# Gated cross-attention and a quantized feed-forward layer on one core: order of the value matrices, form of the last softmax, place of the row statistics and size of the last norms

## The chip, the core and the metric

The kernel runs on one core of a Trainium2 chip. The metric is the device time of one execution in microseconds (us), as the median of several runs of the same program. A profile is one execution of its own, recorded by the hardware profiler. The engines are named as in the profile: PE is TensorE (matrix multiplications and transposes), DVE is VectorE, ACT is ScalarE, POOL is GpSimd, and SP is SyncE, which issues most of the transfers.

## What is computed

The input `x` has 4 batches of 1024 tokens of 512 features. The context has 64 rows of 512 features for each batch. All data are float32.

```python
def _layernorm(x, axis=-1, eps=1e-05):
    m = jnp.mean(x, axis=axis, keepdims=True)
    v = jnp.var(x, axis=axis, keepdims=True)
    return (x - m) / jnp.sqrt(v + eps)

# cross-attention: 16 heads of 64; scores * 64**-0.5, -10000 where key > query
weights = jax.nn.softmax(scores, axis=-1)
out = jnp.einsum('bhqk,bhkd->bhqd', weights, v)
return out.transpose(0, 2, 1, 3).reshape(bsz, q_len, HEADS * HEAD_DIM) @ w_o

# feed-forward: every act_qdq takes one largest value over the whole tensor
x = act_qdq(x)
up = act_qdq(x @ lpbq_dequant(w_up).T)
gate = act_qdq(x @ lpbq_dequant(w_gate).T)
sig = fixed_qdq_u16(jax.nn.sigmoid(gate))
gate = act_qdq(gate * sig)
o = act_qdq(gate * up)
return o @ lpbq_dequant(w_down).T

x = x + jnp.tanh(g_xattn[0]) * _L0_xattn_ref(_layernorm(x, axis=-1), ctx_1024, ctx_1024, ...)
x = x + jnp.tanh(g_ffn[0]) * _L0_ffn_ref(_layernorm(x, axis=-1), ...)
```

## The kernel before

The 4096 tokens are 32 tiles of 128 rows. Two tiles make a pair `q` (16 pairs, 4 for each batch) and four tiles make a group `g` (8 groups). The keys are folded into the query weights (`m_all`, one matrix for each batch) and the output weights into the values (`vwo`, one for each batch), so that attention for a pair is two products of 512 by 1024 and 1024 by 512. Each product is done by a seven-product scheme of the Strassen kind. The sums that it needs are made on DVE: `batch_sums` for the side of a batch (L398 to L403, four steps over 128x1024 elements), `score_left` for the tokens (L373 to L376) and `weights_turned` for the softmax weights (L665 to L668).

**Set-up (to about 75 us).** The weights are loaded and multiplied, and `m_all` is made for all batches. `value_matrix` (L608) makes a 128x512 piece of `vwo` from two matmuls. Each multiplies 64 rows of context into 64 output rows, and so fills one quarter of the array. For even batches the two lie on the quarters of one diagonal, for odd batches on those of the other. Batches 2 and 3 are made in one loop, a piece of one beside a piece of the other, and stored to DRAM for later. A piece goes from PSUM to SBUF on ACT (L614) or DVE (L616).

**Attention (to about 560 us).** The loop over `q` overlaps pairs. `scores(q + 1)` runs the seven products of the next pair on PE in the order 1, 6, 2, 5, 7, 3, 4. Each result leaves PSUM by an ACT copy (L426) or a DVE addition (L428). After chosen products PE does other work: the transposes of the softmax weights of pair `q` (`turn`, L659, copied by ACT at L661) and the transposes of the centred tokens of pair `q + 2` (`next_left`, L369). Those tokens were centred by ACT (L356) with the mean and deviation of the first norm. For batches 0 and 1 the pieces of `vwo` are made behind products of the first two score blocks: eight pieces of batch 0 during `scores(0)`, eight of batch 1 during `scores(1)`, each time two pieces of the same batch together.

`softmax(q + 1, ...)` follows. For each tile DVE takes the largest score of each head (L444). For the first pair the rest is done in large steps: subtraction (L448), one exponential over 128x1024 (L451), sums (L452). For all others ACT does 16 exponentials, one for each head, with the bias and sum in the instruction (L456). A reciprocal (L461) and a product (L462) end both forms.

`attend(q, ...)` runs seven products for the output in the order 1, 6, 2, 7, 5, 4, 3. They share three PSUM regions, so a product must wait until the result before it in its region was added to `xg` on DVE (L701). Products 6, 7 and 4 follow one another in the region `oq`. At its end the statistics of the two finished tiles are taken (`stats`, L321 and L324).

**Norms.** `norm_of` turns variances into reciprocal deviations. It adds epsilon on DVE (L173), takes a square root on ACT (L176, for which ACT loads another function table), and does six small steps on DVE (L178 to L186). One call can serve a finished group (second norm) and a coming group (first norm) together. For groups 1 to 4 the statistics of the first norm are taken early in set-up; for groups 5, 6 and 7 `group_stats` takes them in the loop at `q` = 7, 9 and 11, and the `norm_of` at the end of that pass uses them.

**After the last pair** the last two tiles are normalized by one `norm_of`, scaled on DVE (L726), their largest value taken (L729) and transposed (L734). The largest value over all tokens (L195 on DVE, L197 across partitions on POOL) gives `inv_x`. Gate and up products (24 units of seven products each), quantization with their own global maxima, and the down projection (from about 1210 us) follow. `token_side` rounds the tokens (L926 and L927 on DVE, L932 and L933 on ACT) and makes the sums of the gate stage (L956 to L965). `weight_sums` (L303 to L306) makes those of the weights: four of six during the last attention, the other two at the call of the first `token_side`.

The order on PE in the loop is the program's. On the other engines a scheduler orders the instructions when the program is built, by its own estimate of times. `tc.high_priority(SOON)` moves an instruction ahead in that order, `tc.issue_after(added)` forbids the instructions in it to stand before the instruction `added`, which is the last addition of `attend`. Each engine then works through its list strictly in order.

## Time and profile before

| quantity | value |
|---|---|
| median of three runs | 1469.01 us (1468.62 to 1470.72) |
| profiled execution | 1470.09 us, of which 1468.3 us are the span of the instructions |
| PE busy | 1423.3 us, 97% of the span |
| DVE busy | 1131.6 us, 77% |
| ACT busy | 688.0 us, 47% |
| mean granted clock of PE | 0.99 |

The span is counted from the first to the last instruction. An entry of a timeline gives its start, its length, engine, line, operation, what it writes and reads, and in brackets how long its engine sat idle before it and what ended that. A matmul in float32 shows as two or more records; the distance from one start to the next tells what it costs. The granted clock is the share of full speed at which PE was allowed to run.

### The profile page before, as it was taken

Reading aid. Unit: us, or ns where it says so; the run is one execution under the profiler, and the core shown is the slowest. Engines: PE = TensorE matmul, PEld = TensorE weight load, DVE = VectorE, ACT = ScalarE, POOL = GpSimd, SP = SyncE. Lnnn points to the kernel's source line nnn. Section 1 sums busy time; section 2 is a strip of 40 time slices with the busy share of each in tenths; the row PEclk is TensorE's granted clock in tenths of the full one; section 3 lists DMA queues with packets and bytes.
Section 4 is the critical chain, followed back from the end, with each engine's and each line's share of the span. In section 5 each row is a group of like instructions: output and inputs, shape, how many; then the busy total and the mean of one; then the engine's idle time right before and its main releaser. Section 6 shows DMA issues by size and latency. Waiting matters only on the chain. (4 is left out here: it accounts for less than half of the span.)

```text
span 1468.3 us, 15353 instructions
## 1 busy us (share of the span) xinstructions
PE 1423.3 (97%) x4944; PEld 863.1 (59%) x4944; DVE 1131.6 (77%) x2071; ACT 688.0 (47%) x1734; POOL 97.5 (7%) x191
## 2 busy tenths in 40 slices
PE   8999999999999988999999999999999899999999
PEld 6636776666676674444444444444444448888887
DVE  2855888988988888799975569888888897666632
ACT  2645777777677562010000049977776532222200
POOL 0000000000000002000000000000000101111110
PEclk9999999999999999999999999999999999999999
DMA  9541232432322235862322439958557474554421
GB/s 329 208 139 41 72 96 91 155 122 69 129 60 85 96 67 212 266 263 86 129 86 108 150 133 343 368 216 314 215 215 258 172 271 173 187 187 173 141 73 44
DMA packets 121402, 240.14 MB, mean 164 GB/s; under 512 B 57700, under 2 KB 57956, under 8 KB 115300
## 3 DMA queue, kind: packets, MB, share of 16 engines
q1 hardware_dynamic: 95844, 137.39, 28.1%
q0 software_dynamic: 18560, 76.56, 13.4%
q10 hardware_dynamic: 6912, 25.17, 4.2%
q8 instruction: 39, 0.64, 0.2%
q14 instruction: 47, 0.39, 0.1%
HBM read 130.03 MB, written 109.05 MB: 163 GB/s over the span
## 5 line engine op out<-in xcount | busy, mean ns | idle before, releaser
L456 ACT ACTIVATE e<-e,mx 128x64 f32<-128x64 f32 x480 | 159.5, 336 | 3.4 <-DVE mx L454 3.3
L863 PE MATMUL pqup<-t,wuT 128*128 128x512 f32 x192 | 92.5, 604 | 5.6 <-DVE raw_up L884 2.7
L428 DVE TENSOR_TENSOR e<-s,e 128x512 f32<-128x512 f32 x80 | 54.8, 685 | 55.2 <-PE s L420 54.9
L420 PE MATMUL s<-t,xs 128*128 128x512 f32 x192 | 91.9, 602 | 2.2 <-DVE xs L374 2.2
L456 ACT ACTIVATION_READ_ACCUMULATOR e<-e,mx 128x1 f32 x480 | 90.9, 189 | 0.0
L879 ACT COPY raw_gate<-ppgate 128x512 f32<-128x512 f32 x24 | 14.0, 585 | 144.7 <-PE ppgate L863 144.7
L1388 PE MATMUL ep<-wdT,upe 128*128 128x256 f32 x336 | 77.1, 379 | 0.0
L1314 ACT ACTIVATE uie<-upe,inv_up 128x1024 int16<-128x1024 f32 x48 | 53.7, 1145 | 48.7 <-DVE upe L1318 28.7
L1388 PE MATMUL eq<-tw,upe 128*128 128x256 f32 x312 | 72.4, 379 | 0.0
L1388 PEld LDWEIGHTS ep<-wdT,upe 128*128 128x128 f32 x336 | 63.8, 190 | 9.1 <-issue 0.5
L1087 ACT ACTIVATE gi<-gt,inv_gate 128x1024 int16<-128x1024 f32 x48 | 54.9, 1143 | 30.0 <-DVE q L1097 29.7
L863 PEld LDWEIGHTS pqup<-t,wuT 128*128 128x128 f32 x192 | 34.5, 189 | 57.8 <-issue 29.7
L863 PE MATMUL ppup<-xu,wuT 128*128 128x512 f32 x144 | 67.7, 592 | 0.0
L693 PE MATMUL oq<-t,eT 128*128 128x256 f32 x256 | 62.3, 387 | 5.2 <-DVE xg L701 5.2
L871 ACT COPY raw_gate<-ppgate 128x512 f32<-128x512 f32 x24 | 14.0, 585 | 108.4 <-PE ppgate L863 77.9
L1388 PEld LDWEIGHTS eq<-tw,upe 128*128 128x128 f32 x312 | 59.3, 190 | 8.1
L1318 DVE SCALAR_TENSOR_TENSOR upe<-uie,inv_o,gse 128x1024 f32<-128x1024 int16 (+1 forms) x50 | 60.5, 1233 | 3.0 <-ACT uie L1314 2.7
L420 PE MATMUL s<-m_all,xs 128*128 128x512 f32 x128 | 59.7, 598 | 1.2 <-DVE vwo L616 0.9
L863 PE MATMUL pqgate<-t,wgTb 128*128 128x512 f32 x128 | 60.4, 594 | 0.0
L420 PEld LDWEIGHTS s<-t,xs 128*128 128x128 f32 x192 | 35.4, 192 | 42.3 <-issue 39.3
L420 PE MATMUL s<-mb,xs 128*128 128x512 f32 x128 | 58.9, 592 | 0.0
L989 DVE TENSOR_REDUCE am_gate<-raw_gate 128x1 f32<-128x1024 f32 x48 | 58.2, 1212 | 0.8
(339 smaller groups left out, 3151.3 us busy)
## 6 DMA issues: line engine op xcount, KB each, us to landing
gate_d<-raw_gate ACTq DMA_DIRECT2D x48, 512.0 KB, 2.6
gt<-gate_d SPq DMA_DIRECT2D x48, 512.0 KB, 4.9
upe<-up_d SPq DMA_DIRECT2D x24, 1024.0 KB, 6.3
up_d<-raw_up POOLq DMA_DIRECT2D x46, 512.0 KB, 3.6
gse<-gsi_d SPq DMA_DIRECT2D x24, 512.0 KB, 4.4
gsi_d<-q SPq DMA_DIRECT2D x44, 256.0 KB, 4.0
xg<-in_x_dram SPq DMA_DIRECT2D x8, 1024.0 KB, 6.5
x_d<-xg POOLq DMA_DIRECT2D x32, 256.0 KB, 2.3
```

What stands on the lines that cost most here:

```text
L420: nc.tensor.matmul(bank[at], a[k][:, h, :], b[k][:, h, :], start=start and h == 0, stop=h == HC // 2 - 1, skip_group_check=True,)
L428: nc.vector.tensor_tensor(dst, bank[at], other, add)
L456: nc.scalar.activation(ei[:, h, :], ei[:, h, :], AF.Exp, bias=mx[:, h : h + 1], accum_out=sm[:, h : h + 1],)
L693: nc.tensor.matmul(bank[at], a[k][:, h, :], b[k][:, h, :], start=start and h == 0, stop=h == HP // 2 - 1, skip_group_check=True,)
L863: nc.tensor.matmul(bank[at], a[k][:, h, :], b[k][:, h, :], start=start and h == 0, stop=h == HC // 2 - 1, skip_group_check=True,)
L871: nc.scalar.copy(r0[:, 1, :], bank["pp"])
L879: nc.scalar.copy(r0[:, 0, :], bank["pp"])
L989: nc.vector.tensor_reduce(am_gate[:, u : u + 1], rf, AX.X, ALU.max, apply_absolute_value=True)
L1087: nc.scalar.activation(gi, g, AF.Copy, scale=inv_g)
L1314: nc.scalar.activation(ui, up[:, i, :], AF.Copy, scale=inv_u)
L1318: ins = nc.vector.scalar_tensor_tensor(o[:, i, w], ui[:, w], c_o, gs[:, i, w], ALU.mult, ALU.mult)
L1388: nc.tensor.matmul(bank[at], a[u // 2][k][:, u % 2, q % 2, :], w_of[u // 2][k][:, u % 2, :], start=start and u == 0, stop=u == UPB - 1, sk ...
```

## The change

Five places are edited. The matrices of batches 0 and 1 are made together, one piece of each at a time, behind five products of `scores(0)` and three of `scores(1)`; the two halves of `batch_sums(0, 1)` and the transposes of pair 1 move accordingly. The softmax of the last tile takes the large steps of the first pair. `group_stats` for groups 5 to 7 comes after the last addition of `attend`. The last two tiles get a `norm_of` each. The last two `weight_sums` for the gate come after the sums of `token_side`.

```diff
@@ softmax
-            if q == 0:
+            if q == 0 or t == NT - 1:
@@ values of batches 0 and 1
-        values_done = [0, 0]
-        def values_of(b, n):
-            def some():
-                for _ in range(n):
-                    hp = values_done[b]
-                    values_done[b] += 1
-                    value_matrix(
-                        b, hp, ps_o.tile([P, H], F32, name=f"ps_vo{b}_{hp}", tag=("opn", "oq")[hp % 2])
-                    )
-            return some
+        values_done = iter(range(HP))
+        def values(then=lambda: None):
+            hp = next(values_done)
+            for b, at in ((0, "opn"), (1, "oq")):
+                value_matrix(b, hp, ps_o.tile([P, H], F32, name=f"ps_vo{b}_{hp}", tag=at))
+            then()
@@ ahead of the loop
-        ahead = scores(0, dict.fromkeys((6, 2, 5, 7), values_of(0, 2)), score_banks(0))
+        ahead = scores(
+            0, {6: values, 2: values, 5: lambda: values(lambda: next_left(1)), 7: values, 3: values},
+            score_banks(0),
+        )
+        softmax(0, ahead)
         firsts = batch_sums(0, 1)
-        next(firsts)
-        softmax(0, ahead)
-        next_left(1)
@@ in the loop, scores of the next pair
-                    behind = {**dict.fromkeys((1, 6, 2, 5), values_of(1, 2)), 3: turn, 4: behind[3]}
+                    behind = {**dict.fromkeys((1, 6, 2), values), 3: turn, 4: behind[3]}
                 ahead = scores(q + 1, behind, score_banks(q + 1))
+                if q == 0:
+                    next(firsts)
                 softmax(q + 1, ahead)
@@ in the loop, around attend
                 load_group(q // 2 + 2)
-                if q // 2 + 2 > 4:
-                    group_stats(pa, q // 2 + 2, xg[q // 2 + 2])
...
             added = attend(q, a[0])
             with tc.issue_after(added):
+                if q % 2 == 1 and 4 < q // 2 + 2 < NG:
+                    group_stats(pa, q // 2 + 2, xg[q // 2 + 2])
                 if b + 1 < B and k in (1, QPB - 1):
                     for _ in batch_sums(b + 1, k // 2):
                         pass
@@ after the loop
-        norm_of(pa, [second_norm(slice(last + 2, NT))], "c2")
+        for t in (NT - 1, NT - 2):
+            norm_of(pa, [second_norm(slice(t, t + 1))], f"c{t}")
+        renormed(NT - 1)
         renormed(NT - 2)
-        renormed(NT - 1)
@@ gate stage
-                nc.vector.tensor_tensor(t[3], x0[:, HI, :], t[1], sub)
+                summed.append(nc.vector.tensor_tensor(t[3], x0[:, HI, :], t[1], sub))
...
-                    for p in range(len(ag), UPB):
-                        ag.append(weight_sums(wgT, sg_t, p, "g"))
+                    with tc.issue_after(summed[-1].ins):
+                        for p in range(len(ag), UPB):
+                            ag.append(weight_sums(wgT, sg_t, p, "g"))
```

More of the change, by code (lines that the diff above doesn't have):

```diff
@@ L923 @@
         with tc.tile_pool(name="pb", bufs=2) as pb:
+            summed = []
             def on_dve(tb, h):
```

## The prediction

> **What bounds the kernel now.** I read the busy times first, then what PE waited for, then the timelines around those waits.

> ```profile
> PE 1423.3 (97%) x4944; PEld 863.1 (59%) x4944; DVE 1131.6 (77%) x2071; ACT 688.0 (47%) x1734; POOL 97.5 (7%) x191
> ```

> PE is the bound, and 45 us of the 1468.3 us span are idle on it. An edit can shorten PE's own work, or remove a wait of PE. The waits of PE from 75 to 600 us (total us, how often, longest) are what the edits aim at:

> ```profile
> PE oq L693 <- DVE xg L701: 5.2, 3, 2.0
> PE ps_xm L734 <- DVE xm L726: 4.1, 1, 4.1
> PE ps_e L659 <- DVE e L462: 3.9, 1, 3.9
> PE ppgate L863 <- ACT xi L932: 2.8, 1, 2.8
> PE s L420 <- DVE xs L374: 2.2, 1, 2.2
> ```

> A wait costs more than its length if the clock drops behind it. Three stretches show when (length, PE busy, granted clock):

> ```profile
> 325.15:328.56 3.41, 1.85 (x9) 1.00 0.60 94
> 441.20:444.60 3.40, 1.41 (x7) 1.00 0.95 133
> 444.60:448.00 3.40, 3.40 (x10) 0.51 0.87 354
> ```

> All times below are on the clock of the profiled execution (span 1468.3 us, 1470.09 us in all, 1.1 us above the median of 1469.01 us). Differences are applied to the median.

> **Values side by side: gain.** The first pair of lines is four pieces, two of batch 2 and two of batch 3. The second is two pieces of one batch.

> ```profile
> 64.28 1.95 PE L608 MATMUL ps_vo<-wo_sb,vT 64*64 64x512 f32 x16
> 66.16 1.09 PE L369 MATMUL ps_xn<-ident,xn 128*128 128x128 f32 x8
> ...
> 78.81 1.93 PE L608 MATMUL ps_vo<-wo_sb,vT 64*64 64x512 f32 x8
> 80.68 1.98 PE L420 MATMUL s<-m_all,xs 128*128 128x512 f32 x4
> ```

> Start to start, four pieces take 1.88 us beside one another and two pieces 1.87 us. Two pieces of different batches thus cost 0.94 us; eight groups save 8 x 0.93 = 7.5 us. The wait on L374 (2.2 us), a short one of 0.2 us and the slow stretch at 103.3 (1.7 us) go too, since the token sums now stand ahead of the softmax on DVE: 11.6 us.

> Two new waits take from this. First, ACT's new order puts the exponential of tile 1 between the two evictions of the sixth group. `scores(1)` would start at 93.9. DVE gets product 3 at 91.2 and does two additions (0.6 us start to start), mask, two maxima and two subtractions (1.15 to 1.2 us): 98.3. The exponential ends at 99.9 and the second eviction (0.65) at 100.6. PE is ready for group seven at 98.5; its halves run at 99.0 and 100.65 and not together, which costs 2.2 us. Second, `batch_sums(0, 1)` now stands on DVE behind L665. From the arrival of the softmax weights (124.29 before) the list is L665, L398, L666, L667, L668, L373, L399: four at 0.60, 1.14, 0.34 and 1.22 us end at 129.4. Product 6 of `attend(0)` needs L399 and is due at 126.05: 3.4 us of wait. Over all phases that loses 0 to 3.4 us of clock, mean 1.9. Part: 11.6 - 2.2 - 3.4 - 1.9 = **4.1 us gained** (2.5 to 6).

> [...]

> **Last softmax in large steps: gain.** PE waits 3.94 us and then runs at half speed:

> ```profile
> 537.85 1.94 PE L659 MATMUL ps_e<-ident,e 128*128 128x128 f32 x8 [3.94 <-DVE e L462]
> ```

> 16 exponentials with their reads (0.33 us start to start, 5.3 us) become one of about 1.0 us, and DVE gets L448 and L452 (1.2 us each). In the new order, exponentials of tile 30 end at 529.9, tile 31's at 530.9. DVE does L462 of tile 30 (to 531.5), L452, an addition, L461, L321, an addition, and L462 (1.22): 535.2. PE waits 1.6 us, which does not drop the clock. Transposes (two times 0.87) and product 1 (1.73) follow, and product 6 of the last `attend` starts at 538.9, not 544.18: **5.3 us gained** (3.5 if the wait passes 2 us).

> **Last norm by tiles, late weight sums: gain.** The added second norm is seven small steps at 0.2 us or less and one square root of 0.2 us. Without four L303 to L306 pairs, and with tile 31's chain begun before the last addition, my walk has the last L729 end at 560.0, not 561.3. The rest of the chain to `inv_x` is unchanged. PE stays idle enough to start the gate slow as now: **1.3 us gained** (0 to 2.5). The moved sums fit before L884, and units 4 and 5 need them 48 us later: nothing. The tokens' L926 and L927 of the next pair also move back and are needed 70 us later: nothing.

> **Statistics behind the additions: loss.** The three waits on L701 go: 2.0, 1.2 and 2.0 us, one with a slow stretch (1.8 us). But what is queued behind the additions is the first norm of the group of two pairs on, and PE needs it soon:

> ```profile
> 328.99 1.99 PE L693 MATMUL oq<-t,eT 128*128 128x256 f32 x8 [1.99 <-DVE xg L701]
> ...
> 338.50 0.16 DVE L173 TENSOR_SCALAR ve_b<-mv 128x4 f32<-128x4 f32 x1
> ...
> 342.27 1.50 ACT L356 ACTIVATE xn<-xg,off,rstd 128x512 f32<-128x512 f32 x2
> ...
> 344.60 1.06 PE L369 MATMUL ps_xn<-ident,xn 128*128 128x128 f32 x8
> ```

> Today the centred tokens end at 343.77, 0.8 us before PE turns them. In the new list, `attend(7)` ends at 330.3 without its wait and the last addition issues at 330.5. DVE then has L398, L461, L321, L462, L324, L428, the first L173, four L321, four L324, L399, L428, L401, L428, L403 before the second L173: five of 1.13, eight of 0.60 and six small ones of 0.08, 10.9 us from 330.9 on, so L173 is at 341.8. ACT's root ends at 342.2; L428 and L444 (1.8 us with their dependence) still stand before L178, at 343.9. The small steps and L665 end at 345.7. ACT has meanwhile loaded the exponential table (1.28 us) and does one exponential first. The first L356 ends at 346.7. PE is ready after six products (1.717) and four transposed blocks (1.74): 342.35. It waits 4.3 us, and product 4 starts at 347.9 where it started at 345.50 before: 2.4 us lost although 2.0 were saved. The same walk loses 3.3 us at `q` = 9 (406.0 for 402.7; there two steps of L233 and L269 stand in the chain) and 0.7 us at `q` = 11 (463.1 for 462.4, which already holds the slow stretch). Each wait of 4.3 to 4.9 us empties over 2 us of some stretch whatever the phase: 1.7 to 3.4 us of clock, mean 2.5, three times. Part: 6.4 + 7.5 = **13.9 us lost** (11 to 17).

> [...]

> **Sum.** 4.1 + 5.3 + 1.3 - 13.9 = -3.2 us: 1469.0 + 3.2 = **1472.2 us**.

> **Rivals.**
> - *The statistics are in time.* PE finds the centred tokens ready at `q` = 7, 9 and 11. Then 5.2 us of waits and 2 us of clock are gained in place of the loss: 10.7 + 7.2 = 17.9, 1451 us. For it speaks that the scheduler put them so by its own estimate; against it, DVE's list would have to be 4.3 us shorter, and its rows vary by less than 0.1 us each. 0.12.
> - *The clock holds.* All waits as above, no slow stretch: 9.4 us better, 1463 us. Against it stand the drops at 2.0 and 2.2 us of idle. 0.04.
> - *The last softmax still drops the clock.* The 1.6 us pass 2 us if tile 30's exponentials or the additions ahead of L452 come 0.4 us later, and two of the four new waits meet two slow stretches: 1.8 + 2.5 more, 1476.5 us. 0.12.

> The pieces not running beside one another would cost 7.5 us more (1480); the first rows above exclude it nearly.

> **How the numbers follow.** My forecast has 0.72. 0.2% (2.9 us) is about what a measurement of this kernel can tell from no change, and the forecast lies at that edge: of its 0.72 I put 0.40 above it, 0.30 within, 0.02 below. With the rivals: faster 0.18, same 0.30, slower 0.52. The forecast alone spans 1467 to 1477; the range 1465.5 to 1477.5 leaves out the two fast rivals and little else.

> **What would show it.** Right: values of 0.94 us per group; a wait of product 6 on L399 near 3.4 us; no wait on L701; three waits of L369 on L356 of 4 to 5 us, each with clock 0.5 behind it; the last L659 wait below 2 us. Wrong: no wait of L369, or DVE idle between the last addition and the second L173.

## The result, and the profile after

| kernel | median, us | range of the executions, us | ratio to before (95% interval) |
|---|---|---|---|
| before | 1468.33 | 1465.23 to 1470.72 | |
| changed | 1470.07 | 1468.31 to 1470.96 | 1.0017 (1.0009 to 1.0025) |

The change makes the kernel slower by about 2.5 us (1.3 to 3.7). The profiled execution of the changed kernel took 1468.6 us, of which 1466.8 us are the span. It is at the low end of its runs, so the stages have to be compared one by one, not the spans.

The busy line of the page after the change:

```profile
PE 1417.9 (97%) x4944; PEld 862.1 (59%) x4944; DVE 1135.3 (77%) x2079; ACT 682.9 (47%) x1704; POOL 96.7 (7%) x191
```

PE's busy time fell by 5.4 us and the time did not. The waits of PE from 75 to 600 us say why (engine and line, what it waited for; total us, how often, longest). Up to L634 the changed file has the old line numbers; the matmuls and additions of `attend` are now L689 and L697, the transposes of the last norm L730, their scaling L722.

```profile
PE ps_xn L369 <- ACT xn L356: 13.6, 3, 4.6
PE oq L689 <- DVE t L399: 3.2, 1, 3.2
...
PE ps_e L655 <- DVE mv L324: 1.2, 1, 1.2
```

The waits on the additions (5.2 us) and the 3.9 us at the last softmax are gone. In their place stand three waits for the centred tokens, 13.6 us, and one on the batch sums, 3.2 us. The first of the three, seen in the timeline of DVE (start, length, engine, line, what is written and read) behind the last addition of `attend(7)`, its large batch sums and norm steps:

```profile
332.34 1.19 DVE L399 TENSOR_TENSOR t<-vb,t 128x1024 f32<-128x1024 f32 x1
335.38 1.21 DVE L401 TENSOR_TENSOR vb<-vb,vb 128x1024 f32<-128x1024 f32 x1
337.19 1.20 DVE L403 TENSOR_TENSOR t<-vb,t 128x1024 f32<-128x1024 f32 x1
338.30 0.17 DVE L173 TENSOR_SCALAR ve_b<-mv 128x4 f32<-128x4 f32 x1
340.30 0.19 DVE L178 RECIPROCAL r_b<-s_b 128x8 f32<-128x8 f32 x1
```

and of PE behind it:

```profile
343.44 1.97 PE L369 MATMUL ps_xn<-ident,xn 128*128 128x128 f32 x8 [4.54 <-ACT xn L356]
345.20 2.40 PE L420 MATMUL s<-t,xs 128*128 128x512 f32 x4
347.44 1.04 PE L730 MATMUL ps_xm<-ident,xm 128*128 128x128 f32 x8
```

`attend(7)` began 3.6 us earlier than in the kernel before, so the predicted 341.8 us for the second L173 and 343.9 us for L178 become 338.2 and 340.3: the list of DVE ran as walked, to 0.1 us. Behind the wait PE is slow: 4.00 us from L369 to L730, where 2.61 us are normal (the run with both sums moved, below).

To compare kernels stage by stage I cut each profiled execution at five points on PE: first product of `scores(0)`, end of `attend(0)`, first product of `attend(14)`, end of `attend(15)`, and second product of the gate stage. The columns take in the kernel before, the changed kernel and those experiments below whose stage is the same but for the edit. Each number is one execution, in us.

| stage | without the edit | with it | difference of means |
|---|---|---|---|
| A: `scores(0)` to end of `attend(0)` (values) | 61.20, 59.55, 59.56, 61.17, 59.56 | 57.32, 57.31, 58.56, 57.32 | -2.6 |
| C: to `attend(14)` (statistics) | 384.37, 384.61, 386.39, 384.36, 382.69, 384.36, 386.07 | 395.94, 393.99 | +10.3 |
| D: to end of `attend(15)` (last softmax) | 33.76, 32.61, 33.64, 32.60, 32.41 | 28.52 four times, 28.53 twice | -4.5 |
| E: to the gate (norms and weight sums) | 12.75, 12.41, 12.74, 12.58 | 11.13, 11.38, 11.02, 11.29, 11.37 | -1.4 |

The sum is +1.8 us. The rows show the same instructions taking times up to 3.7 us apart (C, without the edit). Slow stretches come and go there: the wait of 1.99 us on an addition at `q` = 11 was followed by a product of 3.41 us in the profile before, and by one of 1.99 us in the run with the last norms by tiles.

### The profile page after: what moved, and what is told of

It is laid out like the page before. It is cut to its first block, busy times and chain, and to the rows that moved or that the text cites. A ratio compares the mean times of both kernels' runs of the same rounds, so it can differ in the third digit from the quotient of the medians.

```text
span 1466.8 us, 15347 instructions
## 1 busy us (share of the span) xinstructions
PE 1417.9 (97%) x4944; PEld 862.1 (59%) x4944; DVE 1135.3 (77%) x2079; ACT 682.9 (47%) x1704; POOL 96.7 (7%) x191
## 5 line engine op out<-in xcount | busy, mean ns | idle before, releaser
L456 ACT ACTIVATE e<-e,mx 128x64 f32<-128x64 f32 x464 | 154.4, 339 | 3.4 <-DVE mx L454 3.3
L863 PE MATMUL pqup<-t,wuT 128*128 128x512 f32 x192 | 92.5, 604 | 4.7 <-DVE raw_up L889 1.9
L428 DVE TENSOR_TENSOR e<-s,e 128x512 f32<-128x512 f32 x80 | 54.8, 685 | 53.4 <-PE s L420 53.2
L420 PE MATMUL s<-t,xs 128*128 128x512 f32 x192 | 93.6, 611 | 0.0
L863 PEld LDWEIGHTS pqup<-t,wuT 128*128 128x128 f32 x192 | 34.6, 189 | 56.9 <-issue 29.7
L863 PE MATMUL ppup<-xu,wuT 128*128 128x512 f32 x144 | 67.7, 592 | 0.0
L689 PE MATMUL oq<-t,eT 128*128 128x256 f32 x256 | 62.3, 387 | 3.3 <-DVE t L399 3.2
L420 PEld LDWEIGHTS s<-t,xs 128*128 128x128 f32 x192 | 36.3, 197 | 41.2 <-issue 39.6
L420 PE MATMUL s<-m_all,xs 128*128 128x512 f32 x128 | 59.4, 595 | 0.9 <-DVE vwo L616 0.9
L863 PE MATMUL pqgate<-t,wgTb 128*128 128x512 f32 x128 | 60.2, 592 | 0.0
L657 ACT COPY eT<-ps_e 128x512 f32<-128x512 f32 x64 | 34.3, 588 | 55.1 <-PE ps_e L655 54.9
```

The source lines that it names most:

```text
L420: nc.tensor.matmul(bank[at], a[k][:, h, :], b[k][:, h, :], start=start and h == 0, stop=h == HC // 2 - 1, skip_group_check=True,)
L428: nc.vector.tensor_tensor(dst, bank[at], other, add)
L456: nc.scalar.activation(ei[:, h, :], ei[:, h, :], AF.Exp, bias=mx[:, h : h + 1], accum_out=sm[:, h : h + 1],)
L657: nc.scalar.copy(eT[:, 2 * i + k], ps)
L689: nc.tensor.matmul(bank[at], a[k][:, h, :], b[k][:, h, :], start=start and h == 0, stop=h == HP // 2 - 1, skip_group_check=True,)
L863: nc.tensor.matmul(bank[at], a[k][:, h, :], b[k][:, h, :], start=start and h == 0, stop=h == HC // 2 - 1, skip_group_check=True,)
```

## The experiments

Theory: three parts gain roughly as computed, and the late statistics lose more, since DVE's list between the last addition and the norm makes PE wait for the centred tokens and then run slow. Rivals: the statistics cost little and the gains are smaller than computed; or ACT, not DVE, sets the wait. Every kernel ran five rounds beside the kernel before, whose median was 1468.24 us in the first set of four, 1466.63 in the second, 1467.42 in the third and 1468.08 for the last kernel.

**Statistics back in their old place, the rest of the change kept.**

```diff
                 load_group(q // 2 + 2)
+                if q // 2 + 2 > 4:
+                    group_stats(pa, q // 2 + 2, xg[q // 2 + 2])
...
             with tc.issue_after(added):
-                if q % 2 == 1 and 4 < q // 2 + 2 < NG:
-                    group_stats(pa, q // 2 + 2, xg[q // 2 + 2])
```

> The changed kernel with the statistics of groups 5 to 7 back in front of attend. Theory (the late statistics make PE wait for the centred tokens): the three waits of L369 on L356 (4.54, 4.42, 4.62 us in the changed kernel) go, three waits on the additions of attend of 1 to 2 us come back, and the time falls by 11.6 (difference of the traces) to 13.9 us (prediction) from 1470.1, to 1456 to 1459 us. Rival (the other parts give less than computed, the statistics cost little): 1464 to 1470 us.

Measured: 1458.28 us, ratio 0.9929 (0.9916 to 0.9942). That is 11.8 us less than the changed kernel by the medians, 12.9 by the ratios. The waits of L369 on L356 are gone and those on the additions are back (waits, from 135 to 530 us):

```profile
PE oq L689 <- DVE xg L697: 5.5, 3, 2.3
```

So four of the five edits together are worth 10 us (8.5 to 12.3 by the ratio), and one edit spends them all.

**The statistics alone.** The kernel before, `group_stats` behind the additions.

```diff
-                if q // 2 + 2 > 4:
-                    group_stats(pa, q // 2 + 2, xg[q // 2 + 2])
...
             with tc.issue_after(added):
+                if q % 2 == 1 and 4 < q // 2 + 2 < NG:
+                    group_stats(pa, q // 2 + 2, xg[q // 2 + 2])
```

> The kernel before with only the statistics moved behind the additions. Theory: three waits of L369 on L356 of 4 to 5 us, 11 to 14 us slower than before, 1479 to 1483 us. Rival (the statistics are in time, only the waits on the additions go): 1461 to 1468 us.

Measured: 1477.53 us (1473.04 to 1480.79), ratio 1.0065 (1.0049 to 1.0080), 9.5 us slower. The waits, as expected:

```profile
PE ps_xn L369 <- ACT xn L356: 13.2, 3, 4.5
```

The median is below the expected 1479 to 1483 us. In the profiled execution the clock behind the waits cost less than the prediction had: from L369 to L734 PE took 3.97, 4.09 and 4.10 us at `q` = 7, 9 and 11, 1.4 to 1.5 us over 2.61 each, in place of 2.5. But that execution, at 1473.04 us, is the fastest of the six. Where the others lose up to 7.8 us more no trace shows; their mean granted clock is 0.986 to 0.991, against 0.991 in it.

**The values alone.** The kernel before with the edits of `values_done`, `scores(0)`, `softmax(0)` and `batch_sums(0, 1)`, as in the diff of the change.

> The kernel before with only the value matrices of batches 0 and 1 side by side. Theory: 7.5 us of PE work and 4.1 us of waits and slow clock go, 2.2 us at group seven, 3.3 us of wait for product 6 of attend(0) and about 1.8 us of clock come: 4 us faster, 1463 to 1466 us. Rival (the new waits use up the gain, or the clock behind the new wait drops twice): 1467 to 1469 us.

Measured: 1465.42 us, ratio 0.9980 (0.9971 to 0.9990), 2.9 us faster (1.5 to 4.3), where 4.1 was predicted. One cause for the difference is in stage A of the kernels that don't have the edit. The wait on L374 that the edit removes, in the timeline of PE of the run with the last norm by tiles alone, and of the run with the last softmax alone:

```profile
102.11 3.59 PE L420 MATMUL s<-t,xs 128*128 128x512 f32 x4 [2.17 <-DVE xs L374]
105.63 1.93 PE L608 MATMUL ps_vo<-wo_sb,vT 64*64 64x512 f32 x8
```

```profile
102.11 1.98 PE L420 MATMUL s<-t,xs 128*128 128x512 f32 x4 [2.16 <-DVE xs L374]
104.03 1.93 PE L608 MATMUL ps_vo<-wo_sb,vT 64*64 64x512 f32 x8
```

The same wait at the same time: in one execution the product behind it takes 3.52 us to the next start, in the other 1.92. It is slow in two of five executions (the 61.2 us of stage A), so the slow stretch was worth 0.7 us on average, not the 1.7 that the prediction booked.

**The last softmax alone.**

```diff
-            if q == 0:
+            if q == 0 or t == NT - 1:
```

> The kernel before with only the last tile's softmax in large steps. Theory: the wait ahead of the last transposes falls from 3.94 to 1.2 us and the slow clock behind it goes: 5.2 us faster, 1462 to 1464.5 us. Rival (the clock drops here all the same in some executions): 1464.5 to 1466 us.

Measured: 1462.03 us, ratio 0.9958 (0.9943 to 0.9973), 6.2 us faster. The wait is 1.2 us and stage D is 28.52 us, the same as in the changed kernel.

**The last norms by tiles alone, and the weight sums alone.** Two kernels, since the prediction priced them together.

```diff
-        norm_of(pa, [second_norm(slice(last + 2, NT))], "c2")
+        for t in (NT - 1, NT - 2):
+            norm_of(pa, [second_norm(slice(t, t + 1))], f"c{t}")
+        renormed(NT - 1)
         renormed(NT - 2)
-        renormed(NT - 1)
```

> The kernel before with only the last two norms made tile by tile (the weight sums stay where they were). Theory: the chain from the last transposes' end to the gate is shorter by 1.3 (prediction) to 1.6 us (traces), 1466 to 1467.5 us. Rival (inv_x is set by something else, such as the largest value over the partitions or the token rounding on ACT): 1468 us, no change.

```diff
-                    for p in range(len(ag), UPB):
-                        ag.append(weight_sums(wgT, sg_t, p, "g"))
+                    with tc.issue_after(summed[-1].ins):
+                        for p in range(len(ag), UPB):
+                            ag.append(weight_sums(wgT, sg_t, p, "g"))
```

> The kernel before with only the last two weight sums for the gate moved behind the sums of token_side. Theory (the eight steps L303 to L306 on DVE, 0.33 us each, stand between the steps of the last norm): the chain from the last attend to inv_x is 1.3 to 1.6 us shorter, and the gain of the prediction's third part comes from here, since the norms by tiles alone gave none: 1465 to 1466 us where before is 1466.6. Rival (only both together give it): no change.

Measured: the norms by tiles 1467.34 us, ratio 1.0000 (0.9991 to 1.0009); the weight sums 1464.31 us, ratio 0.9983 (0.9972 to 0.9994). Stage E was 13.07 us for the first and 11.28 for the second. So the norms by tiles alone gain nothing, the rival of that run, and the weight sums alone gain, against their rival. DVE's timeline for the norms by tiles alone, one of many such places:

```profile
555.22 0.15 DVE L180 TENSOR_TENSOR s_c<-s_c,r_c 128x1 f32<-128x1 f32 x1
555.28 0.42 DVE L303 TENSOR_TENSOR sg<-wgTb 128x256 f32<-128x256 f32 x1
555.62 0.15 DVE L181 TENSOR_SCALAR s_c<-s_c 128x1 f32<-128x1 f32 x1
```

and for the weight sums alone:

```profile
553.13 0.16 DVE L180 TENSOR_TENSOR s_c<-s_c,r_c 128x2 f32<-128x2 f32 x1
553.33 0.17 DVE L181 TENSOR_SCALAR s_c<-s_c 128x2 f32<-128x2 f32 x1
553.53 0.17 DVE L185 RECIPROCAL rstd<-s_c 128x2 f32<-128x2 f32 x1
```

A step of the norm follows the last after 0.20 us when nothing lies between, and after 0.40 to 0.46 us with a weight sum between. The whole gain of this part is the weight sums' removal from the chain.

**The batch sums behind the norm, statistics left late.** This takes from DVE's list the large steps that PE does not need soon. `norm_of` returns its last instruction (L186) for it.

```diff
-                if b + 1 < B and k in (1, QPB - 1):
-                    for _ in batch_sums(b + 1, k // 2):
-                        pass
...
-                norm_of(pa, parts, f"b{g}")
+                normed = norm_of(pa, parts, f"b{g}")
+                if 4 < g + 2 < NG:
+                    added = normed.ins
+            with tc.issue_after(added):
+                if b + 1 < B and k in (1, QPB - 1):
+                    for _ in batch_sums(b + 1, k // 2):
+                        pass
```

> The changed kernel, in which at q = 7, 9 and 11 the four batch sums (4 x 1.13 us on DVE) may only be issued behind the last step of the norm (L186), while the statistics stay behind the additions. Theory (what PE waits for is DVE's list between the last addition and L186): the list is 3.4 to 4.5 us shorter, the three waits of L369 on L356 (13.6 us together) fall below 1 us each, the slow clock behind them (5.8 us lost in the changed kernel's trace) goes, and no wait on the additions comes back: 1450 to 1454 us. Rival (ACT sets it: two table loads of 1.28 us, the copies and an exponential ahead of L356): the waits stay above 3 us, 1466 to 1470 us. Second rival (the batch sums are then late for attend of the next batch or push the sums of the softmax weights): a new wait of 2 to 4 us at the next attend, 1456 to 1462 us.

Measured: 1456.49 us, ratio 0.9927 (0.9914 to 0.9940), 12 to 13 us less than the changed kernel against the kernel before of each set. The waits (file lines from L190 on are one higher here):

```profile
PE ps_xn L370 <- ACT xn L357: 3.3, 1, 3.3
...
PE oq L690 <- DVE xg L698: 1.5, 4, 0.5
```

At `q` = 7 and 11 the wait for the centred tokens is gone. ACT's order changed as well: the load of the exponential's table, 1.28 us, stood ahead of the centring (L356) in the changed kernel and stands behind it here. So ACT has to be ruled out by the end of the norm on DVE. At `q` = 7 in the changed kernel (last step of the norm on DVE, then the centring on ACT):

```profile
341.87 0.23 DVE L186 SCALAR_TENSOR_TENSOR off<-mv,rstd 128x4 f32<-128x4 f32 x2
342.59 1.50 ACT L356 ACTIVATE xn<-xg,off,rstd 128x512 f32<-128x512 f32 x2
```

and in this run:

```profile
335.72 0.24 DVE L186 SCALAR_TENSOR_TENSOR off<-mv,rstd 128x4 f32<-128x4 f32 x2
336.64 1.51 ACT L357 ACTIVATE xn<-xg,off,rstd 128x512 f32<-128x512 f32 x2
```

The norm ends 6.1 us earlier and the centring begins 6.0 us earlier, 0.5 to 0.7 us behind it in both. So DVE's list set the wait. No new wait at an `attend` came, as the second rival would have it. The time is above the expected 1450 to 1454 us; one wait of 3.28 us is left at `q` = 9, where the rounding of a gate weight chunk (L228 to L270 in this file) also stands between the statistics and the norm.

**Both sums moved.** On top of that, the first half of `batch_sums(0, 1)` right behind the last value matrices.

```diff
-                    behind = {**dict.fromkeys((1, 6, 2), values), 3: turn, 4: behind[3]}
+                    behind = {1: values, 6: values, 2: lambda: values(lambda: next(firsts)), 3: turn, 4: behind[3]}
...
-                if q == 0:
-                    next(firsts)
```

> As the run with the batch sums behind the norm, and the first half of batch_sums(0, 1) called right behind the last value matrices, so that L398 and L399 stand in front of the additions of scores(1) on DVE. Theory: product 6 of attend(0) no longer waits 3.2 us, and the slow stretch behind it (1.8 us) goes: 4 to 5 us faster than that run, 1446 to 1449 us. Rival (the sums hold up the additions of scores(1), PE waits for its PSUM banks instead): 1449 to 1453 us.

Measured: 1452.91 us, ratio 0.9904 (0.9889 to 0.9918). The wait on L399 is gone and 3.6 us are gained by the medians, less than 4 to 5 and within the rival's range. At group seven the waits on the evictions are longer (PE's timeline):

```profile
99.80 1.08 PE L609 MATMUL ps_vo<-wo_sb,vT 64*64 64x512 f32 x4 [1.53 <-ACT vwo L615]
101.32 1.52 PE L609 MATMUL ps_vo<-wo_sb,vT 64*64 64x512 f32 x4 [0.45 <-ACT vwo L615]
102.77 3.19 PE L421 MATMUL s<-m_all,xs 128*128 128x512 f32 x4
```

The two waits together are 1.98 us, against 0.99 in the run before, and the product behind them runs slow. The cause is on DVE, where the first step of the batch sums (L399 in this file) now stands ahead of the softmax's subtraction (L449):

```profile
92.66 1.22 DVE L399 TENSOR_TENSOR t<-vwo 128x1024 f32<-128x1024 f32 x1
...
95.53 1.21 DVE L449 TENSOR_TENSOR e<-e,mx 128x1024 f32<-128x1024 f32 x1
```

Counted from the start of the product ahead of group seven, the subtraction ends 1.5 us later than in the run before. ACT's first exponential waits for it, and the evictions wait behind the exponential. So the sums did make PE wait for its PSUM banks, as the rival had it, but by way of the softmax and ACT.

**Statistics early and the first batch sums early.**

> The changed kernel with the statistics in front of attend (as in the first run of this study, 1458.3 us) and the first half of batch_sums(0, 1) early. Theory: 4 to 5 us faster than 1458.3, 1453 to 1455 us, and slower than the run with both sums moved by the waits on the additions (5.5 us and one slow stretch of 1.8). Rival: the additions of scores(1) are held up, 1456 to 1460 us.

Measured: 1453.33 us, ratio 0.9903 (0.9888 to 0.9917): 4 to 5 us faster than with the statistics alone put back, and no different from the run above. The four waits on the additions are 5.4 us here, against 3.3 and 1.5 us there. The expectation that this kernel would be the slower one failed: with this order of the sums the place of the statistics no longer shows in the time.

**The chunk behind the norm too.**

```diff
-                turned_chunk(pa, oc, wgT, "g", q < 4)
+                if q == IC - 3:
+                    with tc.issue_after(added):
+                        turned_chunk(pa, oc, wgT, "g", q < 4)
+                else:
+                    turned_chunk(pa, oc, wgT, "g", q < 4)
```

> As the run with both sums moved (1452.9 us), and at q = 9 the rounding of a gate weight chunk (L227 to L269, on DVE between the statistics and the norm) may also only be issued behind the norm. Theory: the last wait of L369 on L356 (3.28 us at q = 9) and the slow clock behind it (1.2 us) go: 1448 to 1450 us. Rival (the chunk or the batch sums then delay the softmax weights' sums): no change or slower, 1452 to 1455 us.

Measured: 1453.28 us, ratio 0.9903 (0.9889 to 0.9918), no gain, as the rival had it, but the wait is not the rival's. The wait for the centred tokens is gone, and one pass later an addition of `attend(10)` is late by as much (PE's timeline):

```profile
406.74 3.23 PE L690 MATMUL oq<-t,eT 128*128 128x256 f32 x8 [3.20 <-DVE xg L698]
```

DVE had been busy without a break from 387.7 us to 408.7 us. So a step pushed back there only chose which of its readers waits.

**The evictions of the values first on ACT.**

```diff
-                nc.scalar.activation(dst, ps, AF.Copy, scale=tanh_g[0])
+                if b < 2:
+                    with tc.high_priority(SOON):
+                        nc.scalar.activation(dst, ps, AF.Copy, scale=tanh_g[0])
+                else:
+                    nc.scalar.activation(dst, ps, AF.Copy, scale=tanh_g[0])
```

> As the run with the chunk behind the norm too, and the evictions of the value pieces of batches 0 and 1 moved ahead of the second exponential of the first pair on ACT. Theory (the exponential between the evictions holds up group seven): of the 1.5 and 0.45 us of waits on L614 at group seven the second goes and the first stays (table load and first exponential ahead of it), 0.4 to 1 us faster, and a stretch of slow clock may go with it: 1446 to 1449 us. Rival (the later exponential delays the first pair's weights and so the additions of scores(1)): no change.

Measured: 1452.13 us (1450.39 to 1452.26), ratio 0.9898 (0.9884 to 0.9913). One wait of 1.53 us is left at group seven. The product behind it takes 1.92 us to the next start, not the 3.12 of the run with both sums moved; but in the run with the chunk behind the norm it took 1.92 us too, behind waits of 1.52 and 0.45 us, so that the full speed is not the edit's doing. The 1446 to 1449 us are not reached. This is the fastest kernel of the study, 15 us below before by the ratio, but its interval overlaps those of the three before it, and its own gain is not shown.

**The batch sums of the score side one pass later.**

```diff
-                if b + 1 < B and k in (1, QPB - 1):
-                    for _ in batch_sums(b + 1, k // 2):
+                if b + 1 < B and k in (2, QPB - 1):
+                    for _ in batch_sums(b + 1, k // 3):
```

> As the run with the evictions moved (1452.1 us), and the batch sums of the score side (L398 to L403 for m_all of the next batch) made one pass later, behind the additions of attend at q = 2, 6 and 10 in place of 1, 5 and 9; they are first needed two passes on. Theory (DVE is full from the norm at q = 9 to attend(10), so that whatever is pushed behind the norm makes an addition of attend(10) late): the wait of 3.2 us on that addition goes with the slow clock behind it (2.0 us), 1446 to 1449 us. Rival (the sums meet full passes at q = 2, 6 or 10 too and the wait moves on once more): 1450 to 1454 us, with a new wait of over 2 us in one of those passes or the next.

Measured: 1455.29 us, ratio 0.9917 (0.9903 to 0.9932), slower by 3 us, though the two intervals overlap a little. The expectation was wrong on a fact of the code: `scores(12)` runs in pass 11, one pass after the sums, not two.

```profile
PE s L421 <- DVE t L400: 7.5, 3, 3.4
```

The wait on the addition of `attend(10)` went, down to 0.5 us at most for all additions, but three products of scores now wait for the sums, 3.40, 1.66 and 2.49 us at 188, 302 and 417 us.

## Why the prediction was right, and where it was not

The forecast was 1472.2 us, 3.2 us slower than before; measured are 1470.07 us and +2.5 us by the ratio. Its likeliest case held, and so did its mechanism: with the statistics put back the kernel is 10 us faster than before, and with the batch sums taken out of DVE's list ahead of the norm the waits at `q` = 7 and 11 go. The three priced rivals did not hold: the statistics are not in time, the clock does not hold, and the last softmax did not drop it in any profile with the edit.

- **Values: 4.1 us predicted, 2.9 (1.5 to 4.3) measured, 2.6 between the means of stage A.** The two new waits came as walked: group seven is split by waits of 0.54 and 0.45 us, which puts the product behind it 2.1 us back where 2.2 was predicted, and product 6 of `attend(0)` waits 3.23 us on L399 where 3.4 was predicted. Two terms were too large. The pieces of one group take 1.02 us where 0.94 was predicted, about 0.7 us over eight groups. And the prediction took means over the phase for the waits that it added, but for the wait that it removed it booked the slow stretch of the one profile in full, 1.7 us. It occurs in two of five executions, 0.7 us. With both put right the sum is 2.4 us.

```profile
79.07 1.09 PE L608 MATMUL ps_vo<-wo_sb,vT 64*64 64x512 f32 x8
80.09 1.98 PE L420 MATMUL s<-m_all,xs 128*128 128x512 f32 x4
...
101.34 1.08 PE L608 MATMUL ps_vo<-wo_sb,vT 64*64 64x512 f32 x4 [0.45 <-ACT vwo L614]
...
120.63 3.49 PE L689 MATMUL oq<-t,eT 128*128 128x256 f32 x8 [3.23 <-DVE t L399]
```

- **Last softmax: 5.3 us predicted, 6.2 (4.0 to 8.4) measured**, 5.24 between the profiles of before and changed. The wait is 1.21 us, not 1.6.
- **Last norm and weight sums: 1.3 us predicted, 1.4 in stage E.** The size is right; the working gave part of it to tile 31's earlier chain, and that part gave nothing by itself. The gain is the weight sums' alone.
- **Statistics: 13.9 us lost by prediction; 11.8 (12.9 by the ratios, give or take about 2 us) between the changed kernel and the one with them put back, 9.5 (7.2 to 11.7) alone.** The waits of 4.54, 4.42 and 4.62 us are those of the walk (4.3 to 4.9); its list for `q` = 7 has seven small steps where it counts six, less than 0.1 us. The clock term, 2.5 us for each wait, is larger than the two profiles show. In five of six such waits PE lost 1.4 to 1.5 us: one slow stretch, the first 0.4 to 0.7 us of which PE still spent waiting in the changed kernel. Only at `q` = 11 of the changed kernel did two slow stretches follow (windows from start to end; their length, then the busy time of PE, PEld, DVE, ACT and POOL, then the granted clock, and two figures of the DMA):

```profile
342.90:346.30 3.40, 2.86 (x10) 2.34 (x11) 1.98 (x4) 3.40 (x6) 0.00 (x0) 0.51 0.00 0
346.30:349.70 3.40, 3.40 (x18) 2.48 (x18) 3.33 (x7) 3.40 (x11) 0.00 (x0) 1.00 0.00 0
...
465.30:468.70 3.40, 2.25 (x9) 2.10 (x10) 2.57 (x6) 3.40 (x7) 0.00 (x0) 0.56 0.00 0
468.70:472.10 3.40, 3.40 (x7) 1.38 (x6) 2.35 (x6) 3.18 (x10) 0.00 (x0) 0.50 0.00 0
```

  At `q` = 7, 9 and 11 that is 1.4, 1.5 and 3.0 us in the changed kernel, 4.3 us in all in the run of the statistics alone: a mean of 5.1 for the three, where the prediction had 7.5. But these are two draws of the phase, not six. The three waits of one execution end 61.2 to 61.8 us apart, and the drops of the clock behind them in the changed kernel (342.83, 404.27 and 465.71 us) are 61.44 us apart, 18 stretches of 3.41 us, so that all three meet nearly the same phase. Both profiles are also among the faster executions of their kernels. Whether 2.5 us is too much as a mean over the phase is not shown.

That the total was nearer than its terms is in part luck. The other four edits gain 10.4 us together, by the run with the statistics put back, where 10.7 was predicted; in it the values came out about 1 us below and the last softmax about 1 us above, each within its interval. The loss was 1 to 4 us below the predicted one. The single edits do not add up exactly: by their ratios they sum to -2.1 us, against +2.5 for the whole change, with about 4 us of uncertainty in the sum. Where the waits of each kernel fall among the slow stretches could make that difference; no run isolates it, and it stays open.

The prediction's reading of the slow clock, fixed stretches of 3.41 us in which 2.0 us of idle time bring half speed and 1.6 us do not, fits the profiles in the length of the stretches. In the changed kernel the granted clock drops at 120.97, 342.83, 404.27, 465.71 and 561.29 us, whole multiples of 3.41 us apart, for 3.41 or 6.83 us, as the drops named in the prediction do. In the run with the last norms by tiles the slow products at the gate reach from 557.2 to 566.8 us, waits between them included. The limit does not fit everywhere. During set-up half speed, from 58.93 us in the kernel before and from 59.53 us in the changed one, came after 3.41 us with 1.75 and 1.36 us of idle time, and in the kernel before the stretch from 536.80 us, itself at half speed, had 1.05 us of it and was followed by another. PE was busy for 1.41 of the 3.40 us ahead of the drop at 444.6 in the kernel before. The same 2.16 us of idle time was followed by half speed in some executions and by full speed in others, and 1.98 us, in two waits, were enough in the run with both sums moved. The copies out of PSUM held up PE at one group of eight, by the 0.54 and 0.45 us of group seven in the changed kernel, and there because ACT had an exponential of 1.06 us between two evictions.

## What to carry to other kernels

Before a step is moved behind another, list everything that will stand in its engine's list between that step and its reader; here 4.5 us of batch sums that nobody needed soon turned a removed wait of 2 us into one of 4.5, and holding them back gave 12 to 13 us. Where DVE had no idle time, pushing work back only chose who waits, so the next reader has to be walked too: with the chunk pushed back a wait of 3.28 us became another of 3.20, and with the sums one pass later three waits of 7.5 us in all came. Price the clock as a mean over its phase for waits removed as well as for waits added: one profile shows one phase, and the three waits of the changed kernel, nearly 18 stretches of 3.41 us apart, were all followed by a drop.

## What the runs showed of the hardware

- Half speed of PE did not follow every idle time of about 2 us: the same wait of 2.16 us cost 1.6 us of clock in two of five executions and nothing in three. That its place among the stretches of 3.41 us decides is an estimate from the drops of the two profiles. Each wait of 3.2 to 4.6 us on L356, on L399 and on the addition of `attend(10)` was followed by it.
- A pair of pieces on two quarters of the array beside the other pair costs 1.02 us between full-array products, not 0.94, and the full-array products next to them took 1.81 and 1.91 us from start to start, where the gate's products of the same shape take 1.72.
